# A decoder layer in one kernel: the per-sequence steps after the cross softmax in another order, and the gate's constants set ahead of them

## The chip, the cores and the metric

The kernel runs on one core of one Trainium2 chip. The metric is the device time of one execution in microseconds (us); the time of the kernel before is 736.42 us, the median of three runs (734.47 to 736.47). A core has engines with a queue of instructions each: TensorE (PE; its weight loads are listed as PEld), VectorE (DVE), ScalarE (ACT), GpSimd (POOL) and SyncE (SP, which issues the transfers). Each engine works through its queue in order, and an instruction that waits for another engine holds up everything behind it in its own queue.

## The reference

The input is eight sequences of 128 tokens of 512 numbers. One post-norm decoder layer is computed in float32: self-attention with 4-bit weights, cross-attention, and a feed-forward with low-rank experts chosen by a gate.

```python
x = _layernorm(x + _L0_attn_ref(x, ...))
x = _layernorm(x + _L0_xattn_ref(x, ctx_4096, ctx_4096, ..., 16))
x = _layernorm(x + _L0_ffn_ref(x, ...))
```

What the change touches lies in the second and third line. In the cross-attention the softmax runs over axis 0 of the scores, that is, over all sequences and heads, not over the keys:

```python
scores = jnp.einsum('bqd,bkd->bqk', Q, K) / jnp.sqrt(hd)
attn = jax.nn.softmax(scores, axis=0)
res = jnp.einsum('bqk,bkd->bqd', attn, V)
```

In the feed-forward every token goes through one 512x512 matrix (`main`) and through the two best of eight experts of rank 16; the gate has a small hidden layer with a normalisation of its own:

```python
h = xf @ gw1.T + gb1
h = relu(normalise(h) * ln_gamma + ln_beta)
gates = h @ gw2.T + gb2
top_v, top_i = jax.lax.top_k(gates, 2)
top_g = softmax(top_v)
onehot = (top_i[..., None] == arange(8))
allowed = (onehot.sum(axis=0) <= capacity)
out = xf @ weight.T + lora(xf, onehot, top_g, allowed)
```

## The kernel before

The first 600 us or so compute the self-attention and the cross-attention's projections, scores and exponentials. The change doesn't touch them. What follows is a loop over the eight sequences (called batches here, 0 to 7) in L1319 to L1345, and after it an ending written out in `END_SEQ` (L70).

The cross softmax leaves the exponentials of all scores in tiles `E` (one quarter per `m` = 0 to 3, with all batches in it), and factors in `gmax` and `lmax` that still have to be multiplied in. `weigh(b, m, engine)` (L1080) does that for one batch and one quarter: m 0 and 1 on VectorE, m 2 and 3 on GpSimd. Batches 0 and 1 are weighed ahead of the loop (L1218 to L1224).

For batch i the loop then does the following. The letter is the one that stands for the step in `AV_SEQ` (L62), the string that sets the order in which the loop issues its steps for one i; `step` (L1294) translates it.

- A, `cross_values(i)` (L1251): 16 matmuls of values and weighed scores into the PSUM bank "sc" (`xav`), and a ScalarE copy to `avs`.
- B, `cross_residual(i)` (L1268): four transposes of `avs` on TensorE (`tr_av`, bank "po"), a VectorE addition to the residual `acc` (L1273), and `normalised` (L214): statistics on VectorE (`bn_x` L190, `mv_x` L193), then three tiny GpSimd instructions of one number a partition: epsilon is added (`rstd_x` L199), the power -1/2 taken (`rstd_x` L200), and the negative mean scaled (`nmr_x` L211). What it returns is the ScalarE instruction that applies the norm (L218).
- L: applies the norm of batch i-1 (`acc` L218).
- X, `turn_x2(i-1)` (L1090): four transposes of the normed batch (`tr_x` L819, bank "tr") and a ScalarE copy to `x2f`.
- P, `gate_in(i-1)` (L1095): four matmuls into bank "av" (`pg` L1098), a ScalarE copy of the low-rank part to `tmp` (L1099; the profile calls the tile `tmp_hT`), a VectorE addition that makes `h` (L1101), and `normalised` for the gate, with the same small instructions named `_g`.
- N: applies the oldest gate norm that waits (ScalarE, `h` L218).
- f: the next of four matmul steps of `main_product` (L1106, `pf` L1111). At the end of iteration i the four of batch i-1 are put into `fill`; they are issued in iteration i+1. Each step counts as two TensorE instructions in the trace.
- W: the next `weigh` for batch i+1, from i = 1 on.
- E: copies a finished main product out of PSUM (`acc` L1280), in iterations 5 to 7.
- G, H, h: for the first four batches, in iteration `GATE_IN` = 5: the transpose of `h` with the relu (`trh` L1122, `tmp_hT` L1123), the gates (`pgate` L1130), and twice `choose` (L1141), which picks the best expert in small VectorE instructions. `GATES` (L63) names the groups of batches and the bank that both `trh` and `pgate` use: "tr" for batches 0 to 3.
- J, K: the same for batches 4 and 5, in iteration 7, in bank "sc".

Letters that mean nothing to `step` (v and d) do nothing, and an f with an empty list does nothing. With four entries in `fill`, one iteration therefore issues L N E W W f f A W X J W f f B K P G H h h. Each of the banks "sc", "tr", "av" and "po" is one buffer; "proj", which holds the main products, has four. The engines' queues hold the instructions in the order in which the program issues them. SP's queue has nothing in the loop.

At the start of iteration 4 (L1322 to L1338) the gate's constants are made: 15 small instructions on GpSimd (`rank`, `ones`, `minus_one`, `places`, `experts` twice, a row of `tmp_hT`) and three on VectorE (`experts`, and `order` twice).

Of the kernel before, what the change touches and what calls it, by code (L numbers as in the profile page):

```python
# [10 lines left out]
F32 = mybir.dt.float32  # L11
# [4 lines left out]
ALU = mybir.AluOpType  # L16
AX = mybir.AxisListType
PSUM = bass.MemoryType.PSUM

P = 128  # L20
B, S, D = 8, 128, 512
# [7 lines left out]
NE, R, TOPK = 8, 16, 2  # L29
GH = 4 * NE  # L30
FW = D + NE * R + GH
CAPACITY = int(3.0 * N / NE)
ALPHA = 1.0 / R
EPS = 1e-5
# [24 lines left out]
WEIGH1_ON = 'vvgg'  # L59
LADD_AT = 4  # L60
GSUM_ON = 'g'
AV_SEQ = 'LNEvvWWfvfAvWXJWffBdfKPGdffHhfffhff'  # L62
GATES = ((0, 4, 'tr'), (4, 2, 'sc'), (6, 1, 'po'), (7, 1, 'tr'))  # L63
GATE_IN = 5
LATE_SOFT = 6
EVACUATE = (5, 6, 7)
# [74 lines left out]
def decoder_kernel(ctx: ExitStack, tc: tile.TileContext, a: dict, out: bass.AP):  # L141
    nc = tc.nc

    const = ctx.enter_context(tc.tile_pool(name="const", bufs=1))
    stat = ctx.enter_context(tc.tile_pool(name="stat", bufs=4))
# [8 lines left out]
    def pool(name, side="left", bufs=1):  # L154
        cm = tc.tile_pool(name=name, bufs=bufs, side=side)
        return cm, cm.__enter__()
# [5 lines left out]
    ident = const.tile([P, P], F32, name="ident")  # L162
# [8 lines left out]
    minus_half = const.tile([P, 1], F32, name="minus_half")  # L171
# [15 lines left out]
    def statistics(x, name, wait=0, aggregations=None):  # L187

        st = stat.tile([P, 6], F32, tag="bn", name=f"bn_{name}")
        nc.vector.bn_stats(st[:], x)  # L190
        mv = stat.tile([P, 2], F32, tag="mv", name=f"mv_{name}")
        if aggregations is None:
            nc.vector.bn_aggr(mv[:], st[:])  # L193
        else:
            aggregations.append(lambda: nc.vector.bn_aggr(mv[:], st[:]))
        rstd = stat.tile([P, 1], F32, tag="rstd", name=f"rstd_{name}")

        def power():
            nc.gpsimd.tensor_scalar(rstd[:], mv[:, 1:2], EPS, None, ALU.add)  # L199
            nc.gpsimd.tensor_tensor(rstd[:], rstd[:], minus_half[:], ALU.pow)  # L200

        if aggregations is None:
            later(wait, power)
        else:
            aggregations.append(power)
        return mv, rstd

    def negated(mv, rstd, name):

        nmr = stat.tile([P, 1], F32, tag="nmr", name=f"nmr_{name}")  # L210
        nc.gpsimd.tensor_scalar(nmr[:], mv[:, 0:1], rstd[:], -1.0, ALU.mult, ALU.mult)  # L211
        return nmr

    def normalised(x, name):  # L214

        mv, rstd = statistics(x, name)
        nmr = negated(mv, rstd, name)
        return lambda: nc.scalar.activation(x, x, AF.Identity, scale=rstd[:], bias=nmr[:])  # L218

    def layernorm(dst, t, tag, wait=0):  # L220
# [8 lines left out]
    def later(n, f, projects=False):  # L229

        if slot[0] == 0 or n == 0:
            return f()
        delayed.append((slot[0] + n, f, projects))
# [312 lines left out]
    xk = {"w": {}}  # L546
# [180 lines left out]
    for s in range(steps):  # L727
# [4 lines left out]
        if w == 0:  # L732
            h = (s + LEAD) // HALF + 1
# [77 lines left out]
    def other_bank(name, shape=(P, 512)):  # L811

        turn_n[0] += 1
        return bank(("sc", "tr", "av", "po")[turn_n[0] % 4], name, shape)

    def transposed(tr, t):

        for kt in range(KT):
            nc.tensor.transpose(tr[:, kt, :], acc[:, t, ts(kt, P)], ident[:])  # L819
        return tr  # L820

    wq_loads = []
    for t in range(B):
# [8 lines left out]
        tr = transposed(other_bank(f"tr_x1{t}", (P, KT, S)), t)  # L832
# [10 lines left out]
    def chunk(hf, m, rg):  # L843
        return (hf * KT + m) * 4 + rg
# [26 lines left out]
    tops, lsum, sums, added, order, at_end = {}, [], {}, {}, list(SUM_ORDER), []  # L871

    def group_of(c):
        return next(i for i in range(GROUPS) if c < FIRST[i + 1])

    def max_of(gi):
        return gmax[:, gi, :] if gi < EARLY else lmax[:, gi - EARLY + 1, :]
# [20 lines left out]
    def across(x, n=HALF):  # L898
        return x.unsqueeze(1).to_broadcast([P, n, S])
# [166 lines left out]
    for kt in range(KT):  # L1066
        diagonal = fw[:, kt, ts(kt, P)]
        nc.gpsimd.tensor_tensor(diagonal, diagonal, ident[:], ALU.add)


    total = ep.tile([P, HALF, S], F32, tag="part", name="total", bufs=1)[:, : 1 + LATE, :]
    nc.vector.tensor_tensor(total, lsum[0][:], lmax[:], ALU.mult)
# [7 lines left out]
    def weigh(b, m, engine):  # L1080
        hf, j = divmod(b, HALF)
        c, end = chunk(hf, m, 0), chunk(hf, m, 0) + 4
        while c < end:
            gi = group_of(c)
            n = min(end, FIRST[gi + 1]) - c
            e = quads[c // 4][:, c % 4 : c % 4 + n, j, :]
            engine.tensor_tensor(e, e, across(max_of(gi), n), ALU.mult)  # L1087
            c += n

    def turn_x2(t):  # L1090
        tr = transposed(bank("tr", f"tr_x2{t}", (P, KT, S)), t)
        x2f[t] = fp.tile([P, KT, S], F32, tag="x2f", name=f"x2f{t}", bufs=3)
        nc.scalar.copy(x2f[t][:], tr[:])
# [121 lines left out]
    def engine_of(m, on=WEIGH_ON):  # L1215
        return nc.vector if on[m] == "v" else nc.gpsimd
# [6 lines left out]
    for m in range(KT):  # L1223
        weigh(1, m, engine_of(m, WEIGH1_ON))  # L1224

    def open_ffn():
        nonlocal fp, tmp, h, hT, onehot, chosen, top, pr, rank, ones, orders, experts, earlier, minus_one
        cm, fp = pool("f")
        shared = xk["work"].tile([P, 2, B, S], F32, tag="ch1", name="tmp_hT")
        tmp = shared[:, 0]  # L1230
        h = fp.tile([P, B, GH], F32, name="h")
        hT = shared[: GH + 1, 1]
        onehot = fp.tile([P, TOPK, B, NE], F32, name="onehot")
        chosen = fp.tile([P, TOPK, B, NE], F32, name="chosen")
        top = fp.tile([P, TOPK, B], F32, name="top")
        pr = fp.tile([P, TOPK, B], F32, name="pr")
        rank = fp.tile([P, NE], F32, name="rank")
        ones = fp.tile([P, P], F32, name="ones")
        orders = [
            fp.tile([P, NE, 2, NE], F32, name="order"),  # L1240
            fp.tile([P, TOPK, NE], F32, name="places"),
        ]
        earlier = fp.tile([P, TOPK, NE], F32, name="earlier")
        minus_one = fp.tile([P, 1], F32, name="minus_one")
        experts = fp.tile([P, TOPK, NE], F32, name="experts")
        return cm

    fp = tmp = h = hT = onehot = chosen = top = pr = rank = ones = orders = experts = earlier = minus_one = f_cm = None
    x2f, apply, norm, fill, avs, pg = {}, {}, {}, [], {}, {}

    def cross_values(i):  # L1251
# [32 lines left out]
    def gate(k, what):  # L1284

        t, n, tag = GATES[k]
        if what == "G":
# [6 lines left out]
    def step(what, i, state):  # L1294
        if what == "L" and i - 1 in apply:
            apply.pop(i - 1)()
        elif what == "W" and 0 < i + 1 < B and i:
            m = state["w"] = state.get("w", -1) + 1
            weigh(i + 1, m, engine_of(m))
        elif what == "A" and i < B:  # L1300
            cross_values(i)
        elif what == "B" and i < B:
            cross_residual(i)
        elif what == "X" and i:
            turn_x2(i - 1)
        elif what == "P" and i:
            norm[i - 1] = gate_in(i - 1)
        elif what == "N" and norm:
            norm.pop(min(norm))()
        elif what in "GHh" and i == GATE_IN:  # L1310
            gate(0, what)
        elif what in "JK" and i == B - 1:
            gate(1, "GH"["JK".index(what)])
        elif what == "E" and i in EVACUATE:
            evacuate(EVACUATE.index(i))
        elif what == "f" and fill:
            fill.pop(0)()

    for i in range(B):  # L1319
        if i == 0:  # L1320
            f_cm = open_ffn()
        if i == GATE_IN - 1:  # L1322
            for e in range(NE):
                nc.gpsimd.memset(rank[:, e : e + 1], float(NE - e))
            nc.gpsimd.memset(ones[:], 1.0)
            nc.gpsimd.memset(minus_one[:], -1.0)
            for k in range(TOPK):
                nc.gpsimd.memset(orders[1][:, k, :], float(k))

            nc.vector.tensor_reduce(  # L1330
                experts[:, 0], ident[:].rearrange("p (e r) -> p e r", r=R), AX.X, ALU.add
            )
            nc.gpsimd.tensor_scalar(experts[:, 1], experts[:, 0], ALPHA, None, ALU.mult)
            nc.gpsimd.tensor_copy(experts[:, 0], experts[:, 1])
            of, other = (rank[:].unsqueeze(i).to_broadcast([P, NE, NE]) for i in (2, 1))
            nc.vector.tensor_tensor(orders[0][:, :, 0, :], other, of, ALU.is_lt)
            nc.vector.tensor_tensor(orders[0][:, :, 1, :], other, of, ALU.is_gt)
            nc.gpsimd.memset(hT[GH : GH + 1], 1.0)  # L1338
        state = {}
        for what in AV_SEQ:  # L1340
            step(what, i, state)
        while fill:
            fill.pop(0)()
        if i:
            fill.extend(main_product(i - 1, "proj"))  # L1345
# [107 lines left out]
    for what in END_SEQ:  # L1453
# [34 lines left out]
        elif what == "w":  # L1488
            k = chosen_k.pop(0)
# [112 lines left out]
```

## Time and profile before

| | |
|---|---|
| median of 3 runs | 736.42 us (734.47 to 736.47) |
| the profiled execution: its own time | 737.73 us |
| its span in the trace | 735.9 us |
| the loop's first product `xav` to the transpose `tr_x` of batch 7 | 635.4 to 702.7 us |
| from there to the end | 33.2 us |
| share of the span: PE, DVE, ACT, POOL busy | 93%, 85%, 51%, 60% |

The shares are means over stages with different limits. In the first 80% of the span PE is nearly always busy; in the loop no engine is, and what counts there is the chain from one batch's norm to the next one's. The start of the ScalarE instruction that applies a batch's norm (`acc` L218) is a good clock for it:

| batch | 0 | 1 | 2 | 3 | 4 | 5 | 6 | 7 |
|---|---|---|---|---|---|---|---|---|
| norm applied at, us | 644.96 | 651.75 | 659.04 | 665.89 | 674.63 | 683.11 | 692.29 | 700.74 |
| since the one before, us | | 6.79 | 7.29 | 6.85 | 8.74 | 8.48 | 9.18 | 8.45 |

### The profile page before, as it was taken

What the parts mean: (1) busy time and instruction counts of PE and PEld (TensorE: products, weight loads), DVE (VectorE), ACT (ScalarE), POOL (GpSimd) and SP (SyncE); (2) the same over time, 40 slices, a digit from 0 to 9 for tenths busy, and PEclk for the clock granted to TensorE, in tenths of its full rate; (3) what the DMA queues carried; (4) which work ended last, traced back from release to release, by engine and by line L of the source; (5) the groups of instructions that cost most, each with busy time, mean ns of one, the idle gap of its engine ahead of it and who ended that gap; (6) DMA issues with size and microseconds to landing.
All of it is one profiled execution on the core that took longest, in us unless ns stands there. A gap on an engine that the chain in (4) does not pass through costs nothing. (4 is left out here: it accounts for less than half of the span.)

```text
span 735.9 us, 12053 instructions
## 1 busy us (share of the span) xinstructions
PE 687.3 (93%) x3762; PEld 545.7 (74%) x3762; DVE 622.2 (85%) x1448; ACT 376.1 (51%) x1018; POOL 443.9 (60%) x434
## 2 busy tenths in 40 slices
PE   7899999999999999999999999999999898488875
PEld 4687788888888888888888888877887666355542
DVE  5989999999999999999999999998444989934555
ACT  4465655555565555465465554547524554132433
POOL 3764756667576775766758666577503566377325
PEclk9999999999999999999999999999999999689987
DMA  8778342443443343343343332163001001100003
GB/s 285 213 198 254 102 110 69 129 106 82 122 122 87 87 121 96 85 128 103 87 108 73 82 88 61 30 185 115 1 1 29 1 1 60 32 1 1 1 1 114
DMA packets 36242, 65.73 MB, mean 89 GB/s; under 512 B 5327, under 2 KB 7503, under 8 KB 36178
## 3 DMA queue, kind: packets, MB, share of 16 engines
q1 hardware_dynamic: 36178, 64.96, 32.0%
q8 instruction: 30, 0.49, 0.3%
q14 instruction: 34, 0.28, 0.1%
HBM read 41.87 MB, written 2.10 MB: 60 GB/s over the span
## 5 line engine op out<-in xcount | busy, mean ns | idle before, releaser
L392 ACT ACTIVATE p<-p,nmx 128x128 f32<-128x128 f32 x256 | 99.8, 391 | 88.8 <-DVE nmx L383 88.8
L310 PE MATMUL ps<-xh,w 128*128 128x512 f32 x336 | 140.8, 419 | 0.4 <-DVE part L320 0.4
L310 PE MATMUL ps<-xl,w 128*128 128x512 f32 x336 | 132.0, 393 | 0.0
L399 POOL TENSOR_TENSOR p<-p,rden 128x512 f32<-128x512 f32 x64 | 68.1, 1064 | 102.6 <-DVE rden L398 79.3
L320 DVE SCALAR_TENSOR_TENSOR part<-ps,scales,part 128x512 f32<-128x512 f32 x168 | 124.8, 743 | 2.0 <-PE ps L310 0.4
L344 POOL TENSOR_TENSOR sw<-sw,tables 128x512 f32<-128x512 f32 x71 | 92.7, 1306 | 50.4 <-DMA sw<-x 34.7
L345 POOL TENSOR_TENSOR q<-t,sw 128x512 f32<-128x512 f32 x62 | 93.6, 1510 | 10.0 <-DVE sw L344 5.0
L343 DVE TENSOR_TENSOR t<-x,tables 128x512 f32<-128x512 f32 x80 | 78.4, 980 | 0.7 <-POOL q L345 0.7
L378 PEld LDWEIGHTS sc<-k,q 128*128 128x128 f32 x512 | 67.0, 191 | 8.4 <-DVE q L345 2.1
L435 PE MATMUL po<-woh,ch 128*128 128x512 f32 x256 | 72.2, 403 | 0.0
L316 ACT ACTIVATE part<-ps,scales 128x512 f32<-128x512 f32 x84 | 57.8, 689 | 28.0 <-PE ps L310 28.0
L310 PEld LDWEIGHTS ps<-xh,w 128*128 128x128 f32 x336 | 63.3, 188 | 11.3 <-DVE part L320 0.6
L310 PEld LDWEIGHTS ps<-xl,w 128*128 128x128 f32 x336 | 63.7, 190 | 10.3
L378 PE MATMUL sc<-k,q 128*128 128x128 f32 x512 | 68.2, 275 | 2.5 <-DVE q L345 1.9
L435 PE MATMUL po<-woh,cl 128*128 128x512 f32 x256 | 69.4, 393 | 0.0
L435 PE MATMUL po<-wol,ch 128*128 128x512 f32 x256 | 69.4, 393 | 0.0
L184 ACT CAST ph<-tr 128x512 fp32r<-128x512 f32 x64 | 37.4, 584 | 53.7 <-PE tr L409 53.5
L383 DVE CUSTOM_DVE_ANT_0 p<-sc,causal 128x128 f32<-128x128 f32 x256 | 58.4, 283 | 0.3 <-PE sc L378 0.3
L320 DVE SCALAR_TENSOR_TENSOR x<-ps,scales,part 128x512 f32<-128x512 f32 x70 | 52.4, 749 | 5.5 <-PE ps L310 0.5
L435 PEld LDWEIGHTS po<-wol,ch 128*128 128x128 f32 x256 | 48.2, 188 | 10.9
L435 PEld LDWEIGHTS po<-woh,cl 128*128 128x128 f32 x256 | 48.1, 188 | 10.8
L435 PEld LDWEIGHTS po<-woh,ch 128*128 128x128 f32 x256 | 45.8, 189 | 8.4
(259 smaller groups left out, 1475.8 us busy)
## 6 DMA issues: line engine op xcount, KB each, us to landing
sw<-x SPq DMA_DIRECT2D x160, 128.0 KB, 2.3
raw<-in_qkv SPq DMA_DIRECT2D x28, 384.0 KB, 3.6
oraw<-in_qw_o SPq DMA_DIRECT2D x32, 256.0 KB, 2.8
osc<-in_scales_o SPq DMA_DIRECT2D x32, 256.0 KB, 3.7
xraw<-in_xT SPq DMA_DIRECT2D x4, 512.0 KB, 5.8
acc<-in_x SPq DMA_DIRECT2D x8, 256.0 KB, 5.4
ctxraw<-in_ctxT SPq DMA_DIRECT2D x2, 1024.0 KB, 7.1
out<-o SPq DMA_DIRECT2D x8, 256.0 KB, 2.0
```

What stands on the lines that cost most here:

```text
L184: nc.scalar.copy(hi, src)
L310: nc.tensor.matmul(ps[:], w[:, kt, ts(j, HD)], x[:, kt, ts(hf, HN)], start=(i == 0), stop=(i == 1))
L316: nc.scalar.activation(p[:], ps[:], AF.Copy, scale=sc)
L320: nc.vector.scalar_tensor_tensor(to, ps[:], sc, parts[0][:], ALU.mult, ALU.add)
L343: later(delay("cos"), lambda: engine("cos").tensor_tensor(seqs(t[:]), seqs(x[:]), table(cos_t[m]), ALU.mult), True)
L344: later(delay("sin"), lambda: engine("sin").tensor_tensor(seqs(sw[:]), seqs(sw[:]), table(sin_t[m]), ALU.mult), True)
L345: later(delay("q"), lambda: engine("q").tensor_tensor(dst, t[:], sw[:], ALU.add), True)
L378: nc.tensor.matmul(sc[:, r, :], t["q"][:, r, ts(j, S)], t["k"][:, ts(j, S)], start=True, stop=True)
L383: nc.vector.tensor_tensor_reduce(out=p[:, r, :], in0=sc[:, r, :], in1=causal[:], scale=-1.0, scalar=3e38, op0=ALU.add, op1=ALU.min, accum_ ...
L392: nc.scalar.activation(p[:, r, :], p[:, r, :], AF.Exp, scale=-1.0, bias=nmx[:, r : r + 1], accum_out=den[:, r : r + 1],)
L399: nc.gpsimd.tensor_tensor(p[:], p[:], rden[:].unsqueeze(2).to_broadcast([P, REP, S]), ALU.mult)
L435: nc.tensor.matmul(po[0][:], c[:, r, :], w[:, r, :], start=(r == 0 and i == 0), stop=(r == REP - 1 and i == 2))
```

## The change

`AV_SEQ` gets another order. With four entries in `fill` it now reads L A H X f N E J B W W h h G f f K f P W W. So the values (A) and the turn of the batch before (X) come ahead of the gate's norm (N), the copies of ScalarE with them; one main-product step instead of two stands between X and B, and the other three between B and P, where none stays for the tail of the iteration. W weighs batch i+2 instead of i+1, from i = 0 on. The gate of the first four batches is spread: G stays in iteration 5, H and both h go to iteration 6, and its bank is "av" instead of "tr".

`normalised`, which both norms of the loop use, adds epsilon on VectorE instead of GpSimd. The ending's norms go through `statistics`, which is as it was, except for the gate norm of batch 7, which goes through `normalised`.

`open_ffn` and the gate's constants move from the loop to a place ahead of the first instruction that uses the finished sums (`total`, L1072 before). The same instructions are issued there. The functions between (`weigh` to `gate_softmax`) only change their line numbers.

```diff
-AV_SEQ = 'LNEvvWWfvfAvWXJWffBdfKPGdffHhfffhff'
-GATES = ((0, 4, 'tr'), (4, 2, 'sc'), (6, 1, 'po'), (7, 1, 'tr'))
+AV_SEQ = 'LAHXfNEJBWWhhGffKfPWW'
+GATES = ((0, 4, 'av'), (4, 2, 'sc'), (6, 1, 'po'), (7, 1, 'tr'))
...
-    def negated(mv, rstd, name):
+    def normalised(x, name):
 
+        st = stat.tile([P, 6], F32, tag="bn", name=f"bn_{name}")
+        nc.vector.bn_stats(st[:], x)
+        mv = stat.tile([P, 2], F32, tag="mv", name=f"mv_{name}")
+        nc.vector.bn_aggr(mv[:], st[:])
+        rstd = stat.tile([P, 1], F32, tag="rstd", name=f"rstd_{name}")
+        nc.vector.tensor_scalar(rstd[:], mv[:, 1:2], EPS, None, ALU.add)
+        nc.gpsimd.tensor_tensor(rstd[:], rstd[:], minus_half[:], ALU.pow)
         nmr = stat.tile([P, 1], F32, tag="nmr", name=f"nmr_{name}")
         nc.gpsimd.tensor_scalar(nmr[:], mv[:, 0:1], rstd[:], -1.0, ALU.mult, ALU.mult)
-        return nmr
-
-    def normalised(x, name):
-
-        mv, rstd = statistics(x, name)
-        nmr = negated(mv, rstd, name)
         return lambda: nc.scalar.activation(x, x, AF.Identity, scale=rstd[:], bias=nmr[:])
...
+    def gate_constants():
+        for e in range(NE):
+            nc.gpsimd.memset(rank[:, e : e + 1], float(NE - e))
+        nc.gpsimd.memset(ones[:], 1.0)
+        nc.gpsimd.memset(minus_one[:], -1.0)
+        for k in range(TOPK):
+            nc.gpsimd.memset(orders[1][:, k, :], float(k))
+
+        nc.vector.tensor_reduce(
+            experts[:, 0], ident[:].rearrange("p (e r) -> p e r", r=R), AX.X, ALU.add
+        )
+        nc.gpsimd.tensor_scalar(experts[:, 1], experts[:, 0], ALPHA, None, ALU.mult)
+        nc.gpsimd.tensor_copy(experts[:, 0], experts[:, 1])
+        of, other = (rank[:].unsqueeze(i).to_broadcast([P, NE, NE]) for i in (2, 1))
+        nc.vector.tensor_tensor(orders[0][:, :, 0, :], other, of, ALU.is_lt)
+        nc.vector.tensor_tensor(orders[0][:, :, 1, :], other, of, ALU.is_gt)
+        nc.gpsimd.memset(hT[GH : GH + 1], 1.0)
+
+    f_cm = open_ffn()
+    gate_constants()
 
     total = ep.tile([P, HALF, S], F32, tag="part", name="total", bufs=1)[:, : 1 + LATE, :]
...
-        elif what == "W" and 0 < i + 1 < B and i:
+        elif what == "W" and i + 2 < B:
             m = state["w"] = state.get("w", -1) + 1
-            weigh(i + 1, m, engine_of(m))
+            weigh(i + 2, m, engine_of(m))
...
-        elif what in "GHh" and i == GATE_IN:
+        elif (what == "G" and i == GATE_IN) or (what in "Hh" and i == GATE_IN + 1):
             gate(0, what)
...
     for i in range(B):
-        if i == 0:
-            f_cm = open_ffn()
-        if i == GATE_IN - 1:
-            for e in range(NE):
-                nc.gpsimd.memset(rank[:, e : e + 1], float(NE - e))
...
         state = {}
         for what in AV_SEQ:
             step(what, i, state)
```

More of the change, by code (lines that the diff above doesn't have):

```diff
@@ L1068, in decoder_kernel, with open_ffn @@
         nc.gpsimd.tensor_tensor(diagonal, diagonal, ident[:], ALU.add)
+    fp = tmp = h = hT = onehot = chosen = top = pr = rank = ones = orders = experts = earlier = minus_one = f_cm = None
+    def open_ffn():
+        nonlocal fp, tmp, h, hT, onehot, chosen, top, pr, rank, ones, orders, experts, earlier, minus_one
+        cm, fp = pool("f")
+        shared = xk["work"].tile([P, 2, B, S], F32, tag="ch1", name="tmp_hT")
+        tmp = shared[:, 0]
+        h = fp.tile([P, B, GH], F32, name="h")
+        hT = shared[: GH + 1, 1]
+        onehot = fp.tile([P, TOPK, B, NE], F32, name="onehot")
+        chosen = fp.tile([P, TOPK, B, NE], F32, name="chosen")
+        top = fp.tile([P, TOPK, B], F32, name="top")
+        pr = fp.tile([P, TOPK, B], F32, name="pr")
+        rank = fp.tile([P, NE], F32, name="rank")
+        ones = fp.tile([P, P], F32, name="ones")
+        orders = [
+            fp.tile([P, NE, 2, NE], F32, name="order"),
+            fp.tile([P, TOPK, NE], F32, name="places"),
+        ]
+        earlier = fp.tile([P, TOPK, NE], F32, name="earlier")
+        minus_one = fp.tile([P, 1], F32, name="minus_one")
+        experts = fp.tile([P, TOPK, NE], F32, name="experts")
+        return cm
+    def gate_constants():
[16 more added lines that the diff above has]
+    gate_constants()
     total = ep.tile([P, HALF, S], F32, tag="part", name="total", bufs=1)[:, : 1 + LATE, :]
@@ L1224, in decoder_kernel @@
         weigh(1, m, engine_of(m, WEIGH1_ON))
[L1226 to L1248, printed above, removed]
     x2f, apply, norm, fill, avs, pg = {}, {}, {}, [], {}, {}
@@ L1319, in decoder_kernel @@
     for i in range(B):
-        if i == 0:
-            f_cm = open_ffn()
-        if i == GATE_IN - 1:
-            for e in range(NE):
-                nc.gpsimd.memset(rank[:, e : e + 1], float(NE - e))
[L1325 to L1338, printed above, removed]
         state = {}
```

## The prediction, made before the changed kernel was run

> **What bounds the kernel now.** I read the busy rows by slice first: PE stands at 9 tenths up to 85% of the span and then falls, so the stage that the change touches (635 us on) is not PE's throughput. There I read the chain that ended last, in order of time. One turn of the loop, from batch 3's norm to batch 4's:
>
> ```profile
> 665.89 0.82 ACT acc L218
> 666.76 0.66 PE tr_x L819 x4
> 667.42 1.72 PE pf L1111 x4
> 669.14 0.45 PE tr_av L1271 x4
> 669.61 0.70 DVE acc L1273
> 670.33 0.71 DVE bn_x L190
> 671.06 0.18 DVE mv_x L193
> ...
> 671.39 1.26 POOL E L1087
> 672.65 0.08 issue
> 672.74 0.55 POOL rstd_x L199
> 673.36 0.87 POOL rstd_x L200
> 674.33 0.28 POOL nmr_x L211
> 674.63 0.82 ACT acc L218
> ```
>
> See that the chain goes round four engines, that two main-product steps (`pf`, 1.72) stand in it between the two transposes, and that in this turn a weighing (`E`) on POOL stood ahead of the norm's three small instructions. POOL was late there because the gate's constants (667.12 to 670.06 in the timeline) had held up its two weighings. This turn took 8.74 us; the one before it, free of that, 6.85.
>
> The timeline of POOL and DVE side by side shows a second wait, here in batches 0 and 1:
>
> ```profile
> 642.86 1.26 DVE L1087 TENSOR_TENSOR E<-E,gmax 128x512 f32<-128x512 f32 x2
> 643.68 0.86 POOL L200 TENSOR_TENSOR rstd_x<-rstd_x,minus_half 128x1 f32<-128x1 f32 x1
> ...
> 650.41 1.26 DVE L1087 TENSOR_TENSOR E<-E,gmax 128x512 f32<-128x512 f32 x2
> 650.53 1.19 POOL L211 TENSOR_SCALAR nmr_x<-mv_x,rstd_x 128x1 f32<-128x1 f32 x1
> ```
>
> The columns are start, duration, engine. Alone the power (L200) takes 0.57 and `nmr` 0.27. Where DVE's pair of weighings had begun, the power ended 0.41 after the pair, the `nmr` 0.05 after it (0.13 at 659.00).
>
> Third, the chain around the gate of the first four batches and around batch 7:
>
> ```profile
> 681.10 0.45 PE trh L1122 x4
> ...
> 681.58 0.78 ACT tmp_hT L1123
> ...
> 682.40 1.05 PE pgate L1130 x8
> 683.45 1.91 PE pf L1111 x4
> ...
> 698.11 1.28 PE pg L1098 x8
> 699.39 3.43 PE pf L1111 x8
> ```
>
> PE stands still while ScalarE makes `tmp_hT`, and everything of batch 6 is behind it (turn of 9.18). After `pg` of batch 6 the ending hangs on PE alone: 3.43 of main product, then `tr_x` of batch 7 at 702.66. So what the change is worth is how much earlier that `tr_x` comes; the 33.2 us behind it have the same instructions in the same order.
>
> **The change part by part.** I chain the rows of this execution; "a" is the start of the ScalarE instruction that applies a norm.
>
> *Constants.* POOL gets its 15 instructions while it idles 11.02 us ahead of 633.48, so they cost it nothing, and their 2.9 us leave turn 4. DVE gets three ahead of `total`, which now starts at 630.90, 0.38 after DVE is free. In iteration 4 they started 0.25 (before a wait), 0.14 and 0.14 apart, about 0.5 in all. Bounds: 0, if the 0.38 hides them, and 0.70 (0.25 + 0.23 + 0.22 with nothing hidden). I take 0.2, near the lower end as most of it falls in the idle time.
>
> *Epsilon on DVE.* The trace has no such operation on a 128x1 column; the nearest row is `pr` L1198 with 0.17, plus 0.04 of hand-over. On POOL it took 0.22 and 0.08. Per norm that is between -0.1 and +0.1; I use 0.21 against 0.30.
>
> *Weighing two batches ahead, right behind epsilon.* It adds nothing, but DVE's pair (1.27) now follows epsilon at once in the queue, in iterations 0 to 5, and the power reaches POOL 0.08 after epsilon's end. The pair starts some 0.08 before that end, as it does behind the gate's `mv_g` (657.61), so it is first. Cost of this new wait from both sides: 0, if the power gets between, and 1.0 (pair's end 1.19 after epsilon, +0.42, instead of 0.08 + 0.57). I take 1.0. [...]
>
> *One `pf` step ahead of B instead of two.* From `tr_x` to DVE's addition takes 2.85 now (659.90 to 662.75) and 1.99 with 0.86 less; the copy of `avs`, no longer behind the gate's norm, ends 1.28 after a, ahead of need.
>
> *A steady turn (batches 2 to 4)* is the longer of two ways. The norm's: 0.87 (apply to `tr_x`) + 1.99 + 0.72 + 0.73 + 0.22 + 0.17 + 1.19 + 0.42 + 0.10 + 0.27 + 0.03 = 6.71; without the pair wait 5.7. ScalarE's: its queue now has the copy of `pg` (batch i-1) ahead of the norm (batch i), and `pg` now stands behind all four `pf` steps: 0.87 + `tr_x` 0.49 + `pf` 0.86 + `tr_av` 0.43 + three `pf` 2.58 + `pg` to its copy 1.29 + copy 0.27 = 6.79. So about 6.8, against 7.29, 6.85 and 8.74. The pipeline is no faster than a clean turn of before; it only spares the collisions. ScalarE's way is the cover of the pair wait: without the wait the turn would be no shorter, and without the cover the wait would cost 6.71 - 5.7 = 1.0 a turn. The two ways are within 0.1 of each other.
>
> *Batches 0 and 1* have no `pf` and no cover: each pays the pair wait, but did before too (0.64 and 0.92). Chaining: batch 0 from DVE's addition at 641.33 + 0.2 to apply at 645.36 (before 644.96), batch 1 6.72 later, 652.08 (651.75). Then 658.9, 665.7, 672.5 (659.04, 665.89, 674.63).
>
> *Turn 5* adds the gate's transposes on PE (0.45): 7.3, apply at 679.8 (683.11). It was 8.48 because PE, after 2.1 us of idling before 675.50, took 3.37 instead of 1.72 for the two `pf`; the collision that made it idle is gone.
>
> *Turn 6* gets a new wait. `pgate` (1.05) stands ahead of `tr_x` (0.85 late), and `pg` of batch 5 needs bank "av", which `choose` still reads. `choose` is behind batch 6's epsilon in DVE's queue: addition at a + 3.7, epsilon ends 5.5, six instructions of 0.23 end 6.9. `pg` is copied 1.3 later, and behind that copy wait ScalarE's norm of batch 6 and, on PE, the values and `tr_x`. Together a + 8.5: 688.3 (692.29). Bounds 7.3 (no wait for the bank) and 9.2 (as now).
>
> *Turn 7*: `trh` waits for the gate norm of batch 5 (ends a + 2.55), then `tr_av`, two `pf`, `pgate` 0.55, one `pf`, `pg`, four `pf` of batch 6: `tr_x` of batch 7 at a + 11.0 = 699.3, against 692.29 + 10.37 = 702.66. So 3.4 us earlier; epsilon of the last gate norm adds 0.1: **3.5 us**. The profiled execution's span of 735.9 becomes 732.4, its own time 737.73 becomes 734.2; against the median of 736.42 that is **732.9**.
>
> SP's queue is unchanged and no transfer moves.
>
> **The rivals.**
>
> *The pair wait is not covered.* If the power loses more than the row says, or ScalarE's way is shorter than the norm's and the two waits add up, turns 1 to 5 come out as turn 2 does today, 7.29: 5 x 0.45 = 2.2 more, 735.1. For it: the two ways are 0.1 apart. Against: a longer ScalarE way hides it. Chance 0.2.
>
> *POOL's weighings run into the next norm; slower.* They now start after the gate's power of the same turn. `h` is added at a, its statistics end 0.9 later, POOL's gate instructions at 1.9, the two weighings (2.5) at 4.4; the next power is due at 4.8, DVE's own pair at 4.6. Today the room is 1.8 (662.78 to 664.62). If they are late by more than this 0.2 to 0.4, DVE's pair and the power block one another as at 671.68, where the pair took 2.12 and the turn 1.89 too much. In four turns (2 to 5) that is 7.6: 740.5. Against: both sides hang on the same `pg`, so a late one shifts both. Chance 0.12.
>
> *More is won.* If `choose` keeps bank "av" no longer than PE needs for its three `pf`, turn 6 is 7.3, 1.2 less: 731.7; and if PE keeps its clock in the ending, where `pa` takes 0.86 an instruction at 716 us instead of 0.43, 1.7 less: 730.0. Chance 0.1.
>
> *It doesn't do what it says* (the order comes out as before): excluded by the instruction lists, where the moves stand as described.
>
> **How the numbers follow.** Forecast 732.9 with 0.58, its own range 731.5 to 734.2. The range reaches from the second best case, 730.0, to 737.5, which takes in the uncovered wait with 0.7 for the constants and turn 6 at 9.2, and leaves out the collision of all four turns. A measurement of this kernel tells 0.3% (2.2 us) from no change. Faster by more: the forecast (all but 0.06 of it) and the third rival, with a little of the first: 0.65. Within: most of the first rival and the rest: 0.21. Slower: the second rival and a tail of the first: 0.14.
>
> **What would show it.** The distances between the ScalarE norms: 6.8 in turns 2 to 4, no 8.7 in turn 4, no `pf` of 3.37 in turn 5, some 8.5 in turn 6; the power (L200) at 1.5 instead of 0.57 in batches 0 to 5; ScalarE's norm released by its own copy of `pg` instead of POOL; `tr_x` of batch 7 near 699. The forecast is wrong if POOL's weighings lie over DVE's, or if PE drops its clock in the thinner first turns.

## The result, and the profile after

The changed kernel takes 734.64 us (median of 20 runs, 731.99 to 736.21), beside 736.85 for the kernel before on the same chip (20 runs, 734.47 to 739.76): a ratio of 0.9968 [0.9956, 0.9980], so 2.2 us less. Predicted were 732.9 and 3.5 us less. The profiled execution took 734.62 us with a span of 732.8. Its clock, the starts of the norms' applications, beside that of before:

| batch | 0 | 1 | 2 | 3 | 4 | 5 | 6 | 7 | `tr_x` of 7 | end |
|---|---|---|---|---|---|---|---|---|---|---|
| before, us | 644.96 | 651.75 | 659.04 | 665.89 | 674.63 | 683.11 | 692.29 | 700.74 | 702.66 | 735.9 |
| after, us | 645.08 | 651.19 | 657.88 | 664.57 | 671.26 | 678.38 | 686.89 | 695.06 | 698.13 | 732.8 |
| turn before, us | | 6.79 | 7.29 | 6.85 | 8.74 | 8.48 | 9.18 | 8.45 | | |
| turn after, us | | 6.11 | 6.69 | 6.69 | 6.69 | 7.12 | 8.51 | 8.17 | | |

Two things are read from it. Up to `tr_x` of batch 7 the new kernel is 4.5 us ahead, 1.0 more than the 3.5 predicted. Behind it the ending, in which no instruction of the path was changed but epsilon's, takes 34.67 us instead of 33.24 and gives 1.4 back.

The same turn as in the prediction's first fence, from the chain that ended last (start, length, what):

```profile
664.57 0.82 ACT acc L219
...
665.44 0.66 PE tr_x L820 x4
666.10 0.86 PE pf L1156 x2
666.96 0.44 PE tr_av L1293 x4
667.39 2.58 PE pf L1156 x6
669.97 1.10 PE pg L1143 x8
...
671.26 0.82 ACT acc L219
```

See that POOL and DVE are gone from the chain: PE works without a gap from the transpose of one batch to `pg`, and ScalarE's copy of that `pg` lets the next norm through. The norm itself is ready earlier (`nmr_x` ends at 670.70) and waits. Idle time of ScalarE ahead of a norm's application that ended with POOL's `nmr_x` was 18.5 us in 8 places, and is 5.8 in 2; idle time ahead of the copy of `pg`, ended by PE, rose from 22.2 to 30.5.

The timeline of DVE and POOL, from two windows that overlap, shows the wait that the prediction priced at 1.0 a turn:

```profile
655.79 1.29 DVE L1132 TENSOR_TENSOR E<-E,gmax 128x512 f32<-128x512 f32 x2
655.96 0.93 POOL L216 TENSOR_TENSOR rstd_x<-rstd_x,minus_half 128x1 f32<-128x1 f32 x1 [0.77 <-DVE rstd_x L215]
656.39 0.69 DVE L1132 TENSOR_TENSOR E<-E,gmax 128x512 f32<-128x512 f32 x1
656.98 0.27 POOL L218 TENSOR_SCALAR nmr_x<-mv_x,rstd_x 128x1 f32<-128x1 f32 x1
```

The first row covers both weighings, the third the second of them alone, 0.69 long and up to 657.08. The first ends, at the same length, at 656.48. The power ends at 656.89: 0.41 after the first weighing, and ahead of the second's end. So it waited for one weighing only, and lost 0.36 against its 0.57, not 1.0.

The last steps of the loop and the ending, from the chain again:

```profile
685.04 0.20 DVE second L1198
...
685.37 1.34 PE pg L1143 x8
...
698.29 0.45 PE tr_x L820 x4
...
708.11 1.28 PE trt L1387 x6
...
712.48 3.60 PE pa L1414 x4
```

`pg` of batch 5 does wait for `choose` (`second`) to leave bank "av". The `pa` group of the ending takes 0.9 an instruction. The windows of the ending (start:end, length, busy time of PE, PEld, DVE, ACT, POOL with counts, then the granted clock, DMA share, GB/s) tell why:

```profile
705.00:707.50 2.50, 0.33 (x2) 0.24 (x2) 2.25 (x9) 0.25 (x1) 1.78 (x3) 1.00 0.00 0
707.50:710.00 2.50, 2.28 (x10) 1.93 (x11) 1.23 (x2) 1.58 (x4) 1.17 (x1) 0.51 0.00 0
...
712.50:715.00 2.50, 2.50 (x3) 0.97 (x4) 1.57 (x8) 1.11 (x4) 0.00 (x0) 0.50 0.03 7
```

PE idles 2.38 us while the gate norm of batch 7 is made, and then has half its clock for 10.2 us (707.56 to 717.80). In the profiled execution of before the same stretch idled 2.43 us, and the clock fell 1.3 us after it, for 6.8 us.

### The profile page after: what moved, and what is told of

Its sections match the earlier page's. It is cut to its first block, busy times and chain, and to the rows that moved or that the text cites. A ratio compares the mean times of both kernels' runs of the same rounds, so it can differ in the third digit from the quotient of the medians.

```text
span 732.8 us, 12054 instructions
## 1 busy us (share of the span) xinstructions
PE 688.0 (94%) x3762; PEld 547.9 (75%) x3762; DVE 620.6 (85%) x1464; ACT 376.5 (51%) x1018; POOL 440.2 (60%) x418
## 4 chain that ended last, share of the span: by engine, by line
PE 78%; DVE 10%; DMA 4%; ACT 3%; POOL 2%; issue 2%; SPq 1%; DVEq 0%; POOLq 0%; ACTq 0%
PE po L436 23%; PE ps L311 21%; PE sc L379 7%; PE av L421 6%; PE tr L410 4%; PE pf L1156 3%; PE pxk L659 3%; PE pxv L623 2%; DVE top L935 2%; PE ps L297 2%; PE pxq L659 2%; PE tr_x L820 1%; DMA sw<-x 1%; DVE E L946 1%; PE pg L1143 1%
## 5 line engine op out<-in xcount | busy, mean ns | idle before, releaser
L379 PE MATMUL sc<-k,q 128*128 128x128 f32 x512 | 68.2, 275 | 2.4 <-DVE q L346 1.9
L440 DVE TENSOR_TENSOR acc<-acc,po 128x512 f32<-128x512 f32 x64 | 43.6, 681 | 10.5 <-PE po L436 9.8
```

What stands on the lines that cost most here:

```text
L379: nc.tensor.matmul(sc[:, r, :], t["q"][:, r, ts(j, S)], t["k"][:, ts(j, S)], start=True, stop=True)
```

## The experiments

Beside each time stands its ratio to the kernel before on the same chip. The loop begins up to 5.3 us apart from execution to execution (`total` at 629.62 to 634.89 us), so stages are compared by their own lengths: "loop" is from the start of `total` to `tr_x` of batch 7 (before 71.76, after 66.77), "ending" is what follows (33.24, 34.67). Turns are those of the table, 1 to 7.

**The changed kernel once more** (no edit), to see which lengths repeat.

> The changed kernel once more, as the yardstick for the three beside it. Theory A (the time is won by the missing collision on POOL and the clock drop behind it, turns 4 and 5, and partly lost again in the ending, where PE runs at half clock for longer): the turns come out as in the first profile (6.7, 6.7, 6.7, 7.1, 8.5, 8.2 from batch 2 on), batch 7's tr_x about 4 to 5 us earlier than in the kernel before, and the ending (tr_x of batch 7 to the end) is 33.2 to 34.7 us depending on the clock alone. Theory B (the deeper order makes every turn shorter): the same turns. The run decides nothing between them; it tells whether the longer ending is of this kernel or of one execution.

732.56 us (10 runs, 730.13 to 737.3), ratio 0.9942 [0.9922, 0.9962]: 4.2 us less. All seven turns are the same within 0.01, the loop is 66.78, the ending 34.55. `total` starts 0.03 after the sums' last instruction, so the constants ahead of it cost DVE nothing.

**The kernel before once more** (no edit).

> The kernel before once more, for a second look at its ending. Theory E (the ending is 33.2 to 34.7 us by how long PE runs at half clock in it, which shifts from one execution to the next): the turns are those of the first profile within 0.1 us where the clock doesn't differ, the ending anything between 32 and 35, and its length follows the number of TensorE instructions at double duration. Theory F (the change itself made the ending 1.4 us longer): the ending is 33.2 again.

735.28 us (one run). Turns 5.06 9.05 6.86 8.74 6.78 9.18 8.44, loop 70.09, ending 33.16. The chain of turn 4 and the start of turn 5:

```profile
670.76 1.27 POOL E L1087
...
674.01 0.82 ACT acc L218
674.88 0.66 PE tr_x L819 x4
675.54 1.72 PE pf L1111 x4
```

The collision is there (turn 4 again 8.74, the weighing again in the chain), PE idles 2.11 us ahead of `tr_x` in both executions, and yet the two `pf` steps take 1.72 and not 3.37. So the collision of turn 4 alone doesn't decide whether turn 5 runs at half clock: it is 6.78 here and 8.48 in the first execution, which is the whole difference of the two loops. (Turn 2 is longer since the norm ahead of it comes earlier; turns 1 and 2 together are 14.08 and 14.11.)

The windows give the granted clock. In the first execution it is 0.50 from 676.08 to 679.49 us, where the two `pf` steps lie (from 676.00, 3.54 long), and 1.00 in the windows on both sides. Here the same row of the timeline is 1.88 long behind the same idling. What decides between the two no run shows.

**Only the constants early**: the kernel before, with its constants ahead of `total`.

```diff
-        if i == GATE_IN - 1:
-            for e in range(NE): ...
+    f_cm = open_ffn()
+    gate_constants()
     total = ep.tile(...)
```

> The kernel before with only the gate's constants moved ahead of the loop. Theory A: turn 4 falls from 8.74 to 6.9 to 7.3, turn 5 from 8.48 to 6.9 to 7.3 with two pf at 1.72 instead of 3.37, turn 3 may rise to 7.3 as DVE's weighings no longer wait for the constants; together some 2 to 3 us less, most of what the whole change wins (734 to 734.5, ratio 0.996 to 0.997). Theory B: the order is what counts, so this alone wins under 1 us (ratio 0.999 to 1.0).

736.36 us, ratio 0.9991 [0.9979, 1.0004]. Turns 5.86 9.13 7.40 7.41 6.84 9.11 8.45, loop 70.26, ending 34.33. Turn 4 loses its 8.74, but POOL, no longer late, now meets DVE's pair in turns 3 and 4: the power there takes 1.12 instead of 0.57, and turn 3 grows from 6.85 to 7.40. Together the two win 0.8. The wait took the place of the collision; that the constants alone are the gain is refuted.

**Everything but the constants**: the changed kernel, with the constants made at the start of iteration 4.

```diff
-    gate_constants()
...
+        if i == GATE_IN - 1:
+            gate_constants()
         state = {}
```

> The changed kernel with the gate's constants made at the start of iteration 4 again. Theory A: POOL's constants (2.9 us) stand ahead of batch 4's power, DVE's order waits for rank ahead of batch 4's addition; turn 4 rises from 6.7 to about 9.3, PE idles and turn 5 takes two pf at half clock again; 2.5 to 4 us more than the changed kernel, so no gain or next to none over the kernel before (ratio 0.999 to 1.002). Theory B: the deeper order hides them, under 1 us more (ratio 0.997 to 0.998).

734.82 us, ratio 0.9969 [0.9955, 0.9983], beside 0.9942 on the same chip for the change as it is. Turn 4 is 8.33, all others as in the changed kernel, loop 68.34, ending 32.19.

```profile
665.89 2.45 POOL E L1131 x2
668.34 0.25 POOL rank L1096 x8
...
668.97 0.61 DVE acc L1294
```

POOL's first constants stand behind its two weighings, DVE's `order` waits for them, and behind `order` waits the addition to the residual: 1.64 us, all of it in one turn. No half clock follows, though PE idles 1.71 us ahead of `tr_x`: the next six `pf` matmuls take 2.74 in the timeline, as in the changed kernel. So in the new order the early constants are worth 1.6 us, in the old one the 0.8 of turns 3 and 4, which its time doesn't tell from nothing.

**Another bank for the first gates**, to take the wait for `choose` from turn 6.

```diff
-GATES = ((0, 4, 'av'), ...
+GATES = ((0, 4, 'sc'), ...
```

> The changed kernel with the first gates' bank 'sc' instead of 'av', so that pg of batch 5 doesn't wait until choose has read the gates. If that wait is what turn 6 pays, pg starts 0.9 earlier behind the third pf (684.5 instead of 685.4 in the changed kernel's trace), turn 6 falls from 8.5 to 7.5 and the time by 0.9 us (ratio 0.9955 to 0.9965 to the kernel before). Rival: PE's own work in that turn (6.6 plus 0.45 and 1.0 for the gates) leaves no room, turn 6 stays above 8.2.

734.31 us, ratio 0.9963 [0.9947, 0.9978]. Turn 6 is 8.32 instead of 8.51, the loop 66.58, the ending 34.32. The chain:

```profile
678.52 1.05 PE xav L1279 x32
679.60 0.59 ACT avs L1288
680.24 1.06 PE pgate L1175 x8
681.29 0.59 PE tr_x L820 x4
```

`pgate` now waits for ScalarE's copy out of "sc", and `tr_x` behind it. The wait moved to another bank and 0.2 of the 1.2 us was won.

**A quarter of the main product left out** (three steps a batch instead of four), to shorten PE's way and see what is late next.

```diff
-        return [lambda kt=kt: part(kt) for kt in range(KT)]
+        return [lambda kt=kt: part(kt) for kt in range(KT - 1)]
```

> The changed kernel with three of the four main-product steps of each batch; the fourth quarter of the main product is left out of the result. Theory C (a steady turn is set by TensorE's queue and ScalarE's copy of pg behind it; the norm's own way takes 6.16 in the trace of the changed kernel, from 664.57 to the end of nmr at 670.70): the steady turns fall from 6.69 to 6.2, where the norm's way takes over, not to 5.83 (0.86 less). Theory D (the norm's way with its wait for DVE's pair sets the turn, as priced in the prediction at 6.71): the turns stay at 6.7.

726.04 us (one run). Steady turns 6.08 to 6.16 instead of 6.69, though 0.86 of PE's work is gone from each. The timeline shows what ends them now:

```profile
660.90 0.86 POOL L216 TENSOR_TENSOR rstd_x<-rstd_x,minus_half 128x1 f32<-128x1 f32 x1 [0.61 <-DVE rstd_x L215]
661.86 0.27 POOL L218 TENSOR_SCALAR nmr_x<-mv_x,rstd_x 128x1 f32<-128x1 f32 x1
662.16 0.81 ACT L219 ACTIVATE acc<-acc,nmr_x,rstd_x 128x512 f32<-128x512 f32 x1 [0.22 <-DVE h L1146]
```

The application starts 0.03 after `nmr_x` ends (the profile names `h`, which ends no earlier than the application starts, so it can't have been that). The norm's way, with its pair wait, is thus 6.16 long, 0.53 under PE's and ScalarE's 6.69.

**DVE's pair ahead of the residual**, which takes away the pair wait.

```diff
-AV_SEQ = 'LAHXfNEJBWWhhGffKfPWW'
+AV_SEQ = 'LAHXfNEJWWBhhGffKfPWW'
```

> [...] Theory C: the power falls from 0.86 or 0.93 to 0.57 in the steady turns and the norm's way gets 0.3 to 0.4 shorter, but the turn stays at 6.69, as the copy of pg sets it; turn 1, which has no main product, gets some 0.3 shorter, unless DVE's pair and POOL's weighings now lie over one another. Theory D: the steady turns get shorter by what the power gains.

730.11 us (one run). The power takes 0.55 in the steady turns, which are 6.69 as before: the wait was hidden whole. Turn 1, which has no main product beside it, is 0.39 shorter; batch 0's addition, behind the pair now, comes 1.2 later, and the loop is 67.59. The ending is 31.09: PE idles its 2.39 us there too, but behind it the first `pa` group takes 1.96 and not the 3.76 of the changed kernel: no half clock.

**Epsilon back on GpSimd.**

```diff
-        nc.vector.tensor_scalar(rstd[:], mv[:, 1:2], EPS, None, ALU.add)
+        nc.gpsimd.tensor_scalar(rstd[:], mv[:, 1:2], EPS, None, ALU.add)
```

> The changed kernel with epsilon added on GpSimd again. Theory C: the norm's way gets longer by up to 0.3 to 0.6 (one more instruction in GpSimd's queue that DVE's pair can hold up), but the steady turns stay at 6.7; only batches 0 and 1, which have no cover, come 0.1 to 0.5 later. Theory D: every steady turn gets longer.

734.67 us (one run). Steady turns 6.68 to 6.69, batch 0 from its addition to the application 3.63 instead of 3.24, turn 1 6.50 instead of 6.11. Epsilon on GpSimd takes 0.54 to 0.57, where it took 0.22 in the old order: it now meets DVE's pair too, and the power behind it still takes 0.86. Moving it is worth 0.39 in each of the two uncovered batches and nothing in turns 2 to 5. In turn 6 it costs 0.22 (8.51, here 8.29), since `choose` there stands behind epsilon in DVE's queue. Ending 33.38.

**Weighing one batch ahead again**, in the new order.

```diff
-        elif what == "W" and i + 2 < B:
+        elif what == "W" and 0 < i + 1 < B and i:
...
-            weigh(i + 2, m, engine_of(m))
+            weigh(i + 1, m, engine_of(m))
```

> The changed kernel with the weighing one batch ahead again, in the new order. Theory C: GpSimd's two weighings of batch i+1 stand behind the gate's power and end 4.4 after the norm, the values of batch i+1 on TensorE need them; a turn becomes 4.4 + values 1.1 + tr_x 0.5 + pf 0.9 + tr_av 0.4 + three pf 2.6 + pg and its copy 1.5 = 11.4 instead of 6.7, some 25 us in six turns. Rival: TensorE's queue hides it, the turns stay under 8.

772.97 us (one run). Turns 2 to 5 are 11.9 to 13.9, more than expected: the values of the next batch (`xav`) wait for POOL's weighings (665.69 to 668.14), those for the gate's small instructions, those for `pg`, and PE, idle between, has half clock as well (0.86 a `pf` matmul). The loop is 105.76, 39 us longer than with the deeper weighing, so the rest of the new order needs it. What the deeper weighing would be worth in the old order no run shows. Nor were the other moves (A and X ahead of N, one main-product step instead of two ahead of B) tried apart.

**The ending filled**, in the changed kernel: three matmuls into a bank that nobody reads then, while the gate norm of batch 7 is made.

```diff
             norm.pop(7)()
+            warm = bank("av", "warm")
+            for n in (4, 4, 2):
+                nc.tensor.matmul(warm[:, : n * S], ident[:], x2f[7][:, :n, :]..., start=True, stop=True)
             gate(3, "G")
```

> The changed kernel with three more matmuls on TensorE (two of 128x512, one of 128x256, their result is read by nobody) in the ending, ahead of batch 7's trh, where TensorE stands idle for 2.4 us from 705.3 to 707.7. Theory E: TensorE keeps its clock, trt falls from 1.49 to about 0.8 for six, pa from 3.76 to 1.9 for four, and the ending from 34.6 to 31.5 to 33 us; 1.5 to 3 us less than the changed kernel (ratio 0.991 to 0.994 to the kernel before). Theory F: the clock isn't what makes the ending; no gain, or 0.2 us more for the filling.

730.30 us (5 runs, 729.89 to 731.06), ratio 0.9907 [0.9886, 0.9928]: the fastest of the versions that were run more than once. The loop is 66.77 as in the changed kernel, the ending 31.12. Its windows:

```profile
704.20:706.70 2.50, 2.50 (x8) 1.25 (x8) 2.27 (x9) 0.30 (x1) 1.82 (x3) 1.00 0.00 0
...
709.20:711.70 2.50, 2.21 (x9) 1.15 (x9) 1.67 (x9) 1.06 (x3) 0.00 (x0) 1.00 0.04 7
```

2.4 us of work without use, and the clock stays whole: the first `pa` group takes 1.96 instead of 3.76. No work was taken from the ending, so the 3.5 us are the clock's.

**The ending filled in the kernel before**, with the same three lines.

> The kernel before with the same three matmuls in the ending. Theory E: its ending gets as short as that of the filled changed kernel (31.1 to 31.5 instead of 33.2), so it wins 1.5 to 2.5 us over the kernel before, and the two filled kernels differ by what the loop differs, 3.3 to 5 us. Theory F (the filling helps only the changed kernel, whose ending it had made longer): under 1 us, and the difference of the filled kernels is larger than the loop's.

735.74 us (12 runs), ratio 0.9971 [0.9957, 0.9986]; loop 70.44, ending 31.04 (33.24 and 33.16 unfilled). With both endings filled they are alike, and what is left between the kernels is the loop: 70.44 less 66.77 is 3.7 us.

**The ending and two earlier stretches filled**: as above, and eight and four unread matmuls ahead of the loop and of batch 0's `tr_x`.

> The changed kernel with the three matmuls in the ending and idle matmuls in two gaps at the loop's start as well (8 of 128x256 ahead of the first values, 4 ahead of batch 0's tr_x). Theory E: TensorE has its clock back by batch 1, tr_x and tr_av of turn 1 take 1.0 less together, turn 1 falls from 6.1 to 5.1 to 5.4 and the time by up to 1 us below e8 (ratio 0.989 to 0.991). If the gaps left are enough to lose the clock, turn 1 stays at 6.1 or rises by up to 1, as the idle matmuls at half clock hold up tr_x.

732.50 us (6 runs), ratio 0.9922 [0.9904, 0.9940]. Turn 1 falls from 6.11 to 5.46, since batch 0's `tr_x` takes 0.60 instead of 1.12, and the ending is 31.09. But the first filling takes 5.75 us for its 16 instructions, in a slice of the page (622 to 641 us) where the granted clock is 7 tenths, and makes the first `xav` late. No better than the ending filled alone.

## Why the prediction was right, and where its steps failed

*The loop.* Three profiles of the old order give 71.76, 70.09 and 70.44, three of the new one 66.77, 66.78 and 66.77. The gain there is 3.3 to 5.0, for 3.5 predicted. The forecast compared with the first of the old profiles alone; its own loop (631.1 to 699.3, 68.2 us) would win only 1.9 and 2.2 over the other two. The measured loop is 1.4 shorter than that, 0.5 in batch 0 and 0.6 in turn 1, where the pair wait was priced too high.

*Constants on DVE:* 0.2 predicted, 0 measured: `total` still starts 0.03 behind the sums, as before, so the idle time hid them.

*Epsilon on DVE:* predicted within 0.1. Measured is 0.39 in batches 0 and 1, and 0.22 the other way in turn 6. The step failed in comparing the two rows without the pair wait: on GpSimd epsilon meets the pair as well, and takes twice as long.

*The pair wait:* that the power waits for DVE's weighing was right (0.93 against 0.57), the size not. The step "pair's end 1.19 after epsilon, + 0.42" should have been the first weighing's end, about 0.6 after epsilon, + 0.41. The bounds 0 and 1.0 held, the value taken was at the wrong end. In batches 0 and 1, which the prediction gave no cover, that is why turn 1 is 6.11 and not 6.72. The power comes in between two VectorE weighings here, not behind both, and ends 0.41 behind the first, as it did behind the pair in the profile of before.

*A steady turn:* "about 6.8", set by PE and ScalarE with the norm's way 6.71 just under it. Measured 6.69 and 6.16. The cover is therefore 0.5 wide and not 0.1, and the rival in which it fails had less behind it than the 0.2 it was given. Three runs carry this: without the pair wait the turn stays 6.69, with epsilon on GpSimd too, and with PE's way shortened by 0.86 the norm's 6.16 takes over.

*Turn 4:* the collision went, as predicted, but needs both parts. Early constants alone bring the pair wait in its place; the new order alone keeps 1.64 of it.

*Turn 5:* 7.3 predicted, 7.12 measured, for a reason that was half right. The prediction put the 3.37 of the two `pf` to PE's idling behind the collision. In the changed kernel PE doesn't idle there, and none of the eight profiles with the deeper weighing and the whole main product has half clock in turn 5 (in each timeline two `pf` matmuls take 1.02 there and the next six 2.74). But idling isn't enough: the old kernel run again and the old kernel with its ending filled have the collision (turn 4 of 8.74 and 8.73) and 2.1 us of idling, and a turn 5 of 6.78, shorter than the new order's 7.12. The 8.48 that was to be saved is a price that the old kernel paid in one execution of three. Why in that one is not shown.

*Turn 6 and batch 7:* a + 8.5 and a + 11.0 predicted, 8.51 and 11.24 measured, with the wait for `choose` where it was put. "More is won" by another bank fell: the next bank has a wait of its own.

*POOL running into the next norm,* the slower rival: no turn shows it. Steady turns are equal within 0.01.

*The ending:* "33.2 unchanged, less 0.1" is the step that failed. The prediction saw the half clock and counted 1.7 for its absence, but took its length for fixed. It isn't. These are the endings of nearly the same instructions, without filling. The second column is the mean granted clock of the ending. The third is how long PE worked at half clock behind the idle stretch, estimated from the rows of its matmuls: from the first that takes twice as long to the last, and of a group that is slowed in part twice what it takes more than elsewhere:

| profile | granted clock, mean | work at half clock, us | ending, us |
|---|---|---|---|
| changed kernel | 0.78 | 10.1 | 34.67 |
| changed kernel once more | 0.78 | 9.7 | 34.55 |
| first gates in "sc" | 0.77 | 9.2 | 34.32 |
| epsilon on GpSimd | 0.82 | 6.9 | 33.38 |
| constants late | 0.86 | 3.4 | 32.19 |
| pair ahead | 0.90 | none | 31.09 |
| kernel before | 0.82 | 6.8 | 33.24 |
| kernel before once more | 0.81 | 6.7 | 33.16 |
| only constants early (old order) | 0.77 | 9.2 | 34.33 |

(The mean also has the last microseconds in it, where PE has no work and the granted clock is 0.50: from 728.04 in the changed kernel, from 730.69 in the kernel before.)

Behind an idle stretch of 2.38 to 2.43 us that work takes from nothing to 10.1 us, and the ending follows it. The old order has endings of 34.33 too, the new one of 31.09 to 34.67, so the 1.4 that the ending gave back is not shown to be the new order's. That the half clock comes from the idle stretch is shown by filling it: in both kernels, three profiles, it is gone, and the first `pa` group takes 1.96 in each. Why it stays away in one unfilled profile, and why it lasts three times as long in some of the others as in one, with PE busy nearly all the time, stays open.

So a loop 1.0 better than predicted and an ending 1.4 worse than before came out near the forecast. That they did is in part luck: a pair wait priced too high, 3.4 us of half clock in turn 5 that the old kernel doesn't pay each time, and an ending between 31.1 and 34.7 offset one another.

## What to carry to other kernels

A moved wait is worth nothing where it was hidden, and costs little where another way of the same length covers it: write down both ways round the loop, and shorten the one that is longer. An edit can be worth next to nothing alone and 1.6 us beside another, when one wait stands behind the other; try them apart before one of them is credited. When PE idles for some 2 us ahead of a stretch that hangs on it, look at the granted clock behind the gap first, and in more than one profile: three unread matmuls were worth 2 to 4 us here, as the whole reordering was.

## What was not expected of the hardware

An idle stretch of PE of 2.4 us in the ending was followed by 3.4 to 10.1 us of work at half clock in eight of the nine profiles of the table, and by none in one. With matmuls in the stretch the clock stayed at 1.00 (706.70 to 714.20 us in the filled changed kernel).

One and the same kernel pays for a short gap in one execution and not in the next (turn 5 of the old kernel, behind 2.1 us of idling: 8.48 once, 6.78 twice). One profile can therefore credit a change with a cost that the kernel before doesn't pay each time.

GpSimd gets in between two VectorE instructions in one place and not in another. The power that started at 655.96, in the first of two weighings, waited for that one alone; `nmr` of batch 1 in the old kernel (650.53, 1.19 long) started in the first of two as well and ended behind both. What decides it stays open.
